# A decoder layer with a mixture of experts: biases fetched as four rows and spread on VectorE, and a fifth list of blocks

## The chip, the core and the metric

The kernel runs on one core of a Trainium2 chip, as one program with one launch. The metric is the device time of that core in microseconds (us); the time given is the median of three runs. A profile is one execution recorded by the hardware, with start and length of the instructions of each engine: PE (TensorE's matrix products; its weight loads are listed apart as PEld), DVE (VectorE), ACT (ScalarE), POOL (GpSimd) and SP (SyncE, which here only issues transfers).

## The reference

One decoder layer in float32, with a layer norm after each of its three parts:

```python
x = layernorm(x + attention(x))        # causal, 16 heads of 128, D = 512, x is 8 x 112 x 512
x = layernorm(x + cross(x, ctx))       # linear attention over ctx (8 x 375 x 512), sigmoid gate
x = layernorm(x + experts(x))

def experts(h):                        # 896 tokens
    logits = h @ router_weight.T + router_bias          # 8 experts
    top_vals, top_idx = top_k(logits, 2)
    top_w = softmax(top_vals)                           # two scores a token
    gate_up = h @ gate_up_proj[e] + gate_up_bias[e]     # 512 -> 1024
    gate, up = gate_up[..., ::2], gate_up[..., 1::2]
    gate, up = minimum(gate, 7), clip(up, -7, 7)
    act = (up + 1) * gate * sigmoid(1.702 * gate)
    y_e = act @ down_proj[e] + down_proj_bias[e]        # 512 -> 512
    return sum over the token's two experts of score * y_e
```

A gate or up bias is a vector of 512 along the columns, and so is the down bias. In the kernel the tokens lie on the 128 partitions, so each of these vectors is needed in every partition that holds a token of its expert.

## The kernel before, in words

The 896 tokens are seven tiles of 128. The work goes through three phases: the self-attention up to about 400 us, the linear cross-attention up to about 720 us, and the experts from there to the end.

**Routing and lists.** As a tile finishes the cross-attention, `close(t)` adds it to the residual, normalises it, finds its two experts (`route`) and writes its rows by indirect DMA to `store`, a buffer in device memory grouped by expert. `upto` keeps the counts. `list_blocks(i)` is a chain of some twenty small VectorE operations that turns the counts into two lists: which expert each step works on (`es`, and as integers `eb`), and which block of `store` holds its tokens. `LISTS` says after how many tiles a list is made, and for which steps. Before the change there are four: after five tiles for steps 0 to 2, after six for steps 3 and 4, and after all seven for steps 13 to 17 and for steps 5 to 12. A list made early can only name blocks that are already full.

**Steps.** There are 18. Steps 0 to 4 and 13 to 17 each take one block of 128 rows of one expert. Steps 5 to 12 are paired: 64 rows of one expert on partitions 0 to 63 and 64 rows of another on 64 to 127. Weights stand in four lanes of three 1 MB slabs (`slab[3q]`, `+1`, `+2` for gate, up and down). A paired step uses two lanes. A weight is fetched again only if the lane's expert has changed (`cond`, a flag that the lists give for the steps from 5 on).

**One step.** `project(s, st, 0)` multiplies the block by the gate weights (`gups`, L1120), adds the bias on VectorE (L1128), takes the minimum (L1130) and gives it to ScalarE's sigmoid (L1132). `project(s, st, 1)` does the same with the up weights and forms the product `g` (L1135 to L1139). `transposed_block` turns `g` on PE and copies it out of PSUM on ScalarE (`aT`, L1022). `down` multiplies by the down weights (`yps`, L1147), and adds the down bias times the score on VectorE (L1158). `add_token` (L1185) adds the token itself once, and GpSimd scatters the rows to `parts` (L1164). The loop at L1283 weaves two steps together: step s's gate product, the transposes of step s−1's `g` and of step s+1's tokens (`start`), step s's up product, step s−1's down product.

**Order.** From L1063 on, PE, VectorE, ScalarE and SyncE execute in the order in which the program is written. GpSimd's instructions are placed by the framework. `tick()` advances the chains that are in progress (`close(t)`, later `close_tiles()`) by one piece, so the place where a chain is appended sets where its instructions stand in each engine's order.

**SyncE's queue.** All weights and biases go through it, in written order, with at most eight transfers outstanding. Before the change the biases go with the weights: `fetch_inner` (L927) sends the two weights and then a copy of the 4 KB gate and up bias to all 128 (or 64) partitions of one of four places in `biases` (`BIAS_AT`). `fetch_down_bias` (L966) copies the 2 KB down bias to all partitions of one of two tiles. The inner biases carry the weights' condition except in the steps where a fresh copy is always needed.

**The end.** After step 12's scatter SyncE's queue reads back `parts` into `xn` and `seconds` (L1173, 14 loads of 256 KB). `close_tiles` (L1213) adds the two, collects the statistics of each tile, takes the roots, scales and writes the tiles out. Steps 13 to 17 don't add through `parts` but gather what is there (`gather`, L1189) and write their rows themselves (`write`, L1198). `find_again` (L1244) compares the token numbers of the late steps, with a product on PE (`keys`, L1249), so that a row that comes twice is written once.

Of the kernel before, what the change touches and what calls it, by code (L numbers as in the profile page):

```python
# [10 lines left out]
F32 = mybir.dt.float32  # L11
# [28 lines left out]
LISTS = ((5, slice(0, 3)), (6, slice(3, 5)), (NT, slice(13, 18)), (NT, slice(5, 13)))  # L40
# [6 lines left out]
BIAS_AT = [0, 1, 2, 3, 0] + [1, 3] * 4 + [0, 2, 1, 3, 0]  # L47
# [6 lines left out]
def decoder_layer(ctx: ExitStack, tc: tile.TileContext, t_in: dict, out: bass.AP):  # L54
# [463 lines left out]
    def route(t: int):  # L518
# [32 lines left out]
        if t < LISTS[1][0] - 1:  # L551
            yield
# [143 lines left out]
    with tc.tile_pool(name="cross", bufs=2) as cr:  # L696
# [207 lines left out]
        make_room(free, free[:, 16 * SC :])  # L904
        blocks = store.rearrange("(n p) w -> n p w", p=P)
# [21 lines left out]
        def fetch_inner(s: int, parts_=None):  # L927
# [3 lines left out]
            for i in parts_:  # L931
                _, half = part_of(s, i)
                e = listed(0, s, half, ET.SP, E - 1)
                chosen[i] = e, listed(2, s, half, ET.SP, 1) if s >= EARLY else None
            for k, n in enumerate(("wg", "wu")):
# [7 lines left out]
            for i in parts_:  # L943
                on, _ = part_of(s, i)
                e, cond = chosen[i]
                if s >= PAIRED or (s < EARLY + 2 and i == 1):
                    cond = None
                nc.sync.dma_start(
                    out=biases[on, BIAS_AT[s], :],
                    in_=gubs[bass.ds(e, 1), :].broadcast_to([on.stop - on.start, 2 * I]),  # L950
                    cond=cond,
                )
# [11 lines left out]
        downs = {}  # L964

        def fetch_down_bias(s: int):  # L966
            downs[s] = side.tile([P, D], F32, tag="down_bias", name=f"down_bias_{s}", bufs=2)
            for i, (e, _) in experts_of.pop(s).items():
                on, _ = part_of(s, i)
                nc.sync.dma_start(  # L970
                    out=downs[s][on],
                    in_=t_in["db"][bass.ds(e, 1), :].broadcast_to([on.stop - on.start, D]),
                )
# [15 lines left out]
        def close(t: int):  # L989
# [4 lines left out]
            if t < LISTS[1][0] - 1:  # L994
                yield
            yield from route(t)
            if t == LISTS[0][0] - 1:
                list_blocks(0)
                fetch_inner(0)
                fetch_down(0)  # L1000
                fetch_down_bias(0)
                ahead_x.extend(fetch_tokens(s) for s in range(3))
            elif t == LISTS[1][0] - 1:
# [403 lines left out]
```

## Time and profile before

The median of the three runs is 993.99 us (991.0 to 998.91). The profiled execution took 993.77 us. Its span, from the first instruction to the last, is 992.2 us, and 1.6 us lie around it. The mean granted clock of TensorE is 0.976 of full speed.

The table gives the busy time of each engine by stretch, with the granted clock, the share of time in which the DMA engines were busy, and what they moved.

| stretch (us) | what runs there | PE | DVE | ACT | POOL | clock | DMA | GB/s |
|---|---|---|---|---|---|---|---|---|
| 0 to 400 | self-attention | 389.3 | 148.8 | 89.1 | 81.4 | 1.00 | 0.29 | 103 |
| 400 to 675 | cross-attention | 268.9 | 154.6 | 80.1 | 43.6 | 1.00 | 0.11 | 37 |
| 675 to 720 | its end, with routing | 38.9 | 30.7 | 13.9 | 5.6 | 0.95 | 0.51 | 194 |
| 720 to 757 | steps 0 to 2, last lists | 35.2 | 28.0 | 9.1 | 4.5 | 0.92 | 0.90 | 362 |
| 757 to 814 | steps 2 to 6 | 52.0 | 27.4 | 9.2 | 9.9 | 0.94 | 0.98 | 331 |
| 814 to 852 | steps 7 and 8 | 28.8 | 10.9 | 3.2 | 4.2 | 0.91 | 1.02 | 312 |
| 852 to 912 | steps 9 to 13 | 60.0 | 30.3 | 8.0 | 8.9 | 1.00 | 0.89 | 313 |
| 912 to 966 | steps 14 to 16 | 39.3 | 35.7 | 9.3 | 8.5 | 0.87 | 0.84 | 327 |
| 966 to 992 | step 17 and the end | 12.8 | 14.7 | 5.0 | 7.1 | 0.81 | 0.22 | 74 |

An engine's busy time against the length of its stretch says whether it is the one that sets the pace. PE fills 852 to 912 to the last microsecond. In 814 to 852 and in 912 to 966 it does not. Where the granted clock is under 1, part of the stretch ran at half speed. In the page's groups, `L1128 DVE ... x36 | 24.8, 689 | 73.6 <-PE gups L1120 56.6` reads: 36 instructions of line 1128 on VectorE, 24.8 us of busy time together, 689 ns each; VectorE stood idle 73.6 us in all just before them, and 56.6 us of that ended with a `gups` product of PE. Idle time of an engine that is off the critical path costs nothing.

### The profile page before, as it was taken

The numbers are of one execution on the slowest core, as the hardware profiler recorded it, in microseconds if no ns is written. First come the engines' busy times: TensorE is split into PE (matmuls) and PEld (weight loads), VectorE is DVE, ScalarE is ACT, GpSimd is POOL, SyncE is SP. The second block draws the span as 40 slices with busy tenths as digits, with TensorE's granted clock in tenths as the row PEclk, the third lists the DMA queues.
The fourth block names the chain that finished last, engine by engine and source line by source line (L and its number), as shares of the span: only waits on it lengthen the run. The fifth ranks groups of instructions, "written<-read, shape, count | busy, mean of one in ns | idle before, by whom it ended". The sixth has DMA issues, their size and how long they took to land.

```text
span 992.2 us, 10895 instructions
## 1 busy us (share of the span) xinstructions
PE 925.1 (93%) x3915; PEld 468.3 (47%) x3915; DVE 481.1 (48%) x1053; ACT 226.9 (23%) x394; POOL 173.8 (18%) x239
## 2 busy tenths in 40 slices
PE   7998999999999999999999999999797997899944
PEld 3455644466445655654555455554453432334421
DVE  1356511154213552565413667676776443355675
ACT  1132321033102321322222233333231111011022
POOL 3133300032001413120002222220111210111112
PEclk9999999999999999999999999999988999899977
DMA  9994004101011001130001020210898999889961
GB/s 350 344 348 183 1 1 169 43 20 66 0 43 43 1 1 43 43 105 10 22 0 31 8 71 9 75 32 22 318 375 305 351 354 307 260 298 400 398 227 64
DMA packets 39653, 142.35 MB, mean 143 GB/s; under 512 B 4438, under 2 KB 8598, under 8 KB 29744
## 3 DMA queue, kind: packets, MB, share of 16 engines
q1 hardware_dynamic: 34176, 126.34, 35.8%
q0 software_dynamic: 4768, 14.98, 4.3%
q8 instruction: 31, 0.51, 0.2%
q10 hardware_dynamic: 656, 0.35, 0.1%
q14 instruction: 22, 0.18, 0.1%
HBM read 135.74 MB, written 30.06 MB: 167 GB/s over the span
## 4 chain that ended last, share of the span: by engine, by line
PE 61%; DVE 13%; issue 12%; DMA 9%; ACT 2%; POOL 1%; POOLq 0%; SPq 0%; DVEq 0%; ACTq 0%
PE ops L254 10%; PE vps L344 6%; DMA parts<-y,nums 5%; PE zps L452 3%; PE xqps L888 2%; PE xgps L888 2%; DVE z L861 2%; PE sps L404 2%; PE xops L254 1%; DMA down_bias<-in_db_dram 1%; PE pps L444 1%; DVE p L429 1%; PE sumps L823 1%; DVE kf L783 1%; PE kvps_0a L769 1%
## 5 line engine op out<-in xcount | busy, mean ns | idle before, releaser
L1120 PE MATMUL gups<-slab,bT 128*64 128x512 f32 (+1 forms) x416 | 136.2, 603 | 2.6 <-DMA slab<-in_wu_dram 1.4
L254 PE MATMUL ops<-slab,zT 128*128 128x512 f32 x224 | 97.9, 593 | 0.0
L1147 PE MATMUL yps<-slab,aT 128*64 128x512 f32 (+1 forms) x208 | 74.4, 650 | 14.5 <-ACT aT L1022 9.9
L1120 PEld LDWEIGHTS gups<-slab,bT 128*64 128x64 f32 (+1 forms) x416 | 48.7, 160 | 73.2 <-issue 68.8
L254 PEld LDWEIGHTS ops<-slab,zT 128*128 128x128 f32 x224 | 42.0, 190 | 50.3 <-issue 49.5
L292 POOL TENSOR_TENSOR ws<-slab 128x256 f32<-128x256 f32 x16 | 11.7, 729 | 281.0 <-PE qk_5c L308 83.0
L1128 DVE TENSOR_TENSOR gu<-gups,biases 128x512 f32<-128x512 f32 x36 | 24.8, 689 | 73.6 <-PE gups L1120 56.6
L344 PE MATMUL vps<-slab,x0T 128*112 128x512 f32 x128 | 59.2, 618 | 1.0 <-DVE x0T L204 0.8
L1147 PEld LDWEIGHTS yps<-slab,aT 128*64 128x64 f32 (+1 forms) x208 | 27.1, 173 | 55.9 <-issue 38.5
L1132 ACT ACTIVATE sg<-gu 128x512 f32<-128x512 f32 x18 | 11.3, 629 | 171.7 <-DVE gu L1130 171.6
L261 DVE TENSOR_TENSOR xn<-xn,ops 128x512 f32<-128x512 f32 x28 | 19.2, 684 | 55.5 <-PE ops L254 55.5
L1164 POOL DMA_INDIRECT parts<-y,nums x16 | 16.5, 1033 | 158.8 <-DVE y L1185 144.2
L452 PEld LDWEIGHTS zps<-pT,v 112*128 112x128 f32 x256 | 33.5, 192 | 12.3 <-issue 11.2
L459 DVE COPY zT<-zps 128x448 f32<-128x448 f32 x32 | 20.0, 624 | 39.8 <-PE zps L452 39.8
L344 PEld LDWEIGHTS vps<-slab,x0T 128*112 128x112 f32 x128 | 23.0, 185 | 31.7 <-issue 30.0
L428 DVE TENSOR_REDUCE nm<-p 112x4 f32<-112x448 f32 x32 | 19.7, 616 | 30.5 <-POOL p L418 30.5
L452 PE MATMUL zps<-pT,v 112*128 112x112 f32 x256 | 33.4, 273 | 0.0
L254 PE MATMUL xops<-slab,gate 128*128 128x512 f32 x56 | 25.7, 602 | 7.1 <-DVE gate L863 7.1
L580 POOL DMA_INDIRECT store<-xn,rows x14 | 14.0, 999 | 86.9 <-DVE count L620 57.5
L1158 DVE SCALAR_TENSOR_TENSOR y<-down_bias,score,yps 128x512 f32<-128x512 f32 x17 | 12.7, 747 | 32.6 <-PE yps L1147 24.6
L404 PE MATMUL sps<-k,q 128*112 128x112 f32 x256 | 28.0, 262 | 0.0
L412 ACT ACTIVATE p<-sps 112x448 f32<-112x448 f32 x32 | 17.4, 544 | 45.6 <-PE sps L404 45.6
(804 smaller groups left out, 1606.9 us busy)
## 6 DMA issues: line engine op xcount, KB each, us to landing
slab<-in_wg_dram SPq DMA_DIRECT2D x26, 1024.0 KB
slab<-in_wu_dram SPq DMA_DIRECT2D x26, 1024.0 KB
slab<-in_wd_dram SPq DMA_DIRECT2D x26, 1024.0 KB
store<-slab SPq DMA_DIRECT2D x8, 1806.0 KB
cT<-in_ctxT_dram SPq DMA_DIRECT2D x8, 750.0 KB
biases<-gubs SPq DMA_DIRECT2D x10, 512.0 KB
slab<-in_wq_dram SPq DMA_DIRECT2D x4, 1024.0 KB
slab<-in_wk_dram SPq DMA_DIRECT2D x4, 1024.0 KB
```

The lines of the kernel that those rows point to most:

```text
L254: nc.tensor.matmul(ps, aT[:, c, t * P : (t + 1) * P], w[:, c, :], start=(c == 0), stop=(c == C - 1),)
L261: nc.vector.tensor_add(xn[:, t, :], xn[:, t, :], ps)
L344: nc.tensor.matmul(ps[:S, :], xT[:, c, b * S : (b + 1) * S], w[:, c, :], start=(c == 0), stop=(c == C - 1),)
L404: nc.tensor.matmul(ps[:S, i * S : (i + 1) * S], qk["q"][:, rows], qk["k"][:, rows], start=True, stop=True,)
L428: nc.vector.tensor_reduce(nm, p, AX.X, ALU.max, negate=True)
L452: nc.tensor.matmul(zps[:, i * S : (i + 1) * S], v[:, half * 4 + i, hl * DH : (hl + 1) * DH], pT[:, i * S : (i + 1) * S], start=True, stop= ...
L459: nc.vector.tensor_copy(zT[:, hl, half * HALF : (half + 1) * HALF], zps[:, :HALF])
L861: nc.vector.reciprocal(zf, zf)
L888: nc.tensor.matmul(ps[:, :HALF], w[:, c, g * P : (g + 1) * P], xT[:, c, cols], start=(c == 0), stop=(c == C - 1),)
L1120: nc.tensor.matmul(ps[rows_], st["bT"][:, c, rows_], slab[3 * q + k][:, c, :], start=(c == 0), stop=(c == C - 1),)
L1128: nc.vector.tensor_add(a, ps, st["bias"][:, k * I : (k + 1) * I])
L1147: nc.tensor.matmul(ps[rows_], st["aT"][:, c, rows_], slab[3 * q + 2][:, c, :], start=(c == 0), stop=(c == C - 1 and s < STEPS - 1),)
```

## The change

**Biases.** The tables `BIAS_AT` and `downs` go. All biases of step s are now fetched by `fetch_biases(s)`: for each expert of the step one row of 4 KB to two (paired) or four partitions, one in each group of 32 (partitions 0, 32, 64 and 96), and a row of 2 KB likewise. They go into parts of the `biases` tile: two places for inner biases, four for down biases. They carry no condition. `spread_biases(s)` then copies, in place, the first partition of each group of 32 to the other 31, with VectorE's shuffle under a mask of zeros: one instruction on 128x1024 and one on 128x512. Two memsets on GpSimd clear the places when the tile is made, before `prepare_pair(2)`.

**Order of the transfers.** `fetch_inner` no longer sends biases. At the top of loop step s, `fetch_biases(s + 1)` is asked for, ahead of the weights that step s issues; step 0's come after step 1's up weights. The spread for step s + 1 stands at the end of loop step s, step 0's ahead of its first product.

**Lists.** The first list is split: step 0 is listed after four tiles, steps 1 and 2 after five. It is one more chain of 21 VectorE operations. Step 0's weights are asked for with its list, step 1's gate weights with the second, step 1's up weights later. The places where `close` and `route` compare against `LISTS[1]` now compare against `LISTS[2]`, which keeps its meaning (six tiles).

**The closing.** In loop step 15 the chain `close_tiles()` is appended behind `project(s, st, 1)` instead of ahead of the transposes, so its first piece stands behind the second projection of step 15.

PE's and ScalarE's instructions are the same and in the same order. VectorE has 56 more, GpSimd 3 more, and one of its row writes at the end stands two places later.

```diff
-LISTS = ((5, slice(0, 3)), (6, slice(3, 5)), (NT, slice(13, 18)), (NT, slice(5, 13)))
+LISTS = (
+    (4, slice(0, 1)),
+    (5, slice(1, 3)),
+    (6, slice(3, 5)),
+    (NT, slice(13, 18)),
+    (NT, slice(5, 13)),
+)
...
+        nc.gpsimd.memset(biases[:, 0, :], 0.0)
+        nc.gpsimd.memset(free[:, 16 * SC :], 0.0)
...
-            for i in parts_:
-                on, _ = part_of(s, i)
-                e, cond = chosen[i]
-                if s >= PAIRED or (s < EARLY + 2 and i == 1):
-                    cond = None
-                nc.sync.dma_start(
-                    out=biases[on, BIAS_AT[s], :],
-                    in_=gubs[bass.ds(e, 1), :].broadcast_to([on.stop - on.start, 2 * I]),
-                    cond=cond,
-                )
...
-        def fetch_down_bias(s: int):
-            downs[s] = side.tile([P, D], F32, tag="down_bias", name=f"down_bias_{s}", bufs=2)
-            for i, (e, _) in experts_of.pop(s).items():
-                on, _ = part_of(s, i)
-                nc.sync.dma_start(
-                    out=downs[s][on],
-                    in_=t_in["db"][bass.ds(e, 1), :].broadcast_to([on.stop - on.start, D]),
-                )
+        flat = biases.rearrange("p q n -> p (q n)")
+
+        def inner_bias(s: int):
+            return flat[:, s % 2 * 2 * I : (s % 2 + 1) * 2 * I]
+
+        def down_bias(s: int):
+            at = 4 * I + s % 4 * D
+            return flat[:, at : at + D]
+
+        def fetch_biases(s: int):
+            for to, of in ((inner_bias(s), gubs), (down_bias(s), t_in["db"])):
+                for i, (e, _) in experts_of[s].items():
+                    on, _ = part_of(s, i)
+                    to_ = to[on.start : on.stop : XH]
+                    nc.sync.dma_start(
+                        out=to_, in_=of[bass.ds(e, 1), :].broadcast_to(to_.shape)
+                    )
+
+        def spread_biases(s: int):
+            for b in (inner_bias(s), down_bias(s)):
+                nc.vector.stream_shuffle(b, b, [0] * XH)
...
+            for i, (n, steps_) in enumerate(LISTS):
+                if t == n - 1:
+                    list_blocks(i)
+                    if i == 0:
+                        fetch_inner(0)
+                        fetch_down(0)
+                    if i == 1:
+                        fetch_inner(1, of=(0,))
...
                 steps = [start(0, side, "bT")]
-                fetch_inner(1)
+                fetch_inner(1, of=(1,))
+                fetch_biases(0)
                 fetch_down(1)
-                fetch_down_bias(1)
                 fetch_inner(2)
...
+            if s == 0:
+                spread_biases(0)
+            if s + 1 < STEPS:
+                fetch_biases(s + 1)
             if st:
                 project(s, st, 0)
...
-            if s == STEPS - LATE + 2:
-                chains.append(close_tiles())
             if before_:
                 before_["aT"] = transposed_block(f"aT_{s - 1}", before_["g"], moe, "aT")
...
                 project(s, st, 1)
+                if s == STEPS - LATE + 2:
+                    chains.append(close_tiles())
                 tick()
...
                 fetch_next(s - 1, fetch_down)
-                if s + 1 < STEPS:
-                    fetch_down_bias(s + 1)
                 if s + 3 < STEPS:
                     ahead_x.append(fetch_tokens(s + 3))
+            if s + 1 < STEPS:
+                spread_biases(s + 1)
```

More of the change, by code (lines that the diff above doesn't have):

```diff
@@ L46 @@
 LANES += [(1,), (2,), (3,), (0,), (1,)]
-BIAS_AT = [0, 1, 2, 3, 0] + [1, 3] * 4 + [0, 2, 1, 3, 0]
 LN_EPS = 1e-5
@@ L550, in route @@
         yield
-        if t < LISTS[1][0] - 1:
+        if t < LISTS[2][0] - 1:
             yield
@@ L925, in decoder_layer, with fetch_inner @@
         experts_of = {}
-        def fetch_inner(s: int, parts_=None):
+        def fetch_inner(s: int, parts_=None, of=(0, 1)):
             chosen = experts_of.setdefault(s, {})
@@ L931, in fetch_inner @@
             for i in parts_:
+                if i in chosen:
+                    continue
                 _, half = part_of(s, i)
@@ L934, in fetch_inner @@
                 chosen[i] = e, listed(2, s, half, ET.SP, 1) if s >= EARLY else None
-            for k, n in enumerate(("wg", "wu")):
+            for k in of:
+                n = ("wg", "wu")[k]
                 for i in parts_:
@@ L962, in fetch_down @@
                 )
-        downs = {}
-        def fetch_down_bias(s: int):
-            downs[s] = side.tile([P, D], F32, tag="down_bias", name=f"down_bias_{s}", bufs=2)
-            for i, (e, _) in experts_of.pop(s).items():
-                on, _ = part_of(s, i)
-                nc.sync.dma_start(
-                    out=downs[s][on],
-                    in_=t_in["db"][bass.ds(e, 1), :].broadcast_to([on.stop - on.start, D]),
-                )
+        flat = biases.rearrange("p q n -> p (q n)")
[15 more added lines that the diff above has]
+                nc.vector.stream_shuffle(b, b, [0] * XH)
         def fetch_tokens(s: int):
@@ L993, in close @@
             yield
-            if t < LISTS[1][0] - 1:
+            if t < LISTS[2][0] - 1:
                 yield
             yield from route(t)
[L997 to L1003, printed above, removed]
-                list_blocks(1)
-                ahead_x.append(fetch_tokens(3))
-            elif t == NT - 1:
-                list_blocks(2)
-                list_blocks(3)
+            for i, (n, steps_) in enumerate(LISTS):
[6 more added lines that the diff above has]
+                        fetch_inner(1, of=(0,))
+                    if i < 3:
+                        ahead_x.extend(
+                            fetch_tokens(s) for s in range(steps_.start, min(steps_.stop, NQ))
+                        )
         nums = const.tile([P, STEPS], I32, name="nums")
@@ L1027, in start @@
             xb = ahead_x.pop(0)
-            st = {"x": xb, "bias": biases[:, BIAS_AT[s], :]}
+            st = {"x": xb, "bias": inner_bias(s)}
             st["bT"] = transposed_block(f"bT_{s}", xb, *home)
@@ L1158, in down @@
             nc.vector.scalar_tensor_tensor(
-                y, downs.pop(s), st["score"], ps, ALU.mult, ALU.add
+                y, down_bias(s), st["score"], ps, ALU.mult, ALU.add
             )
@@ L1329, in decoder_layer @@
                 nc.vector.scalar_tensor_tensor(
-                    st["sum"], downs[s], st["score"], st["sum"], ALU.mult, ALU.add
+                    st["sum"], down_bias(s), st["score"], st["sum"], ALU.mult, ALU.add
                 )
```

## The prediction

> **What bounds the kernel now.** I read the busy shares first, then the list of waits, then the last 300 us in order of time, engine by engine; in the fences a timeline row is start, length, engine, line, operation, and in brackets the idle time before it with its releaser.
>
> ```profile
> PE 925.1 (93%) x3915; PEld 468.3 (47%) x3915; DVE 481.1 (48%) x1053; ACT 226.9 (23%) x394; POOL 173.8 (18%) x239
> ...
> DVE gu L1128 <- DMA biases<-gubs: 16.9, 3, 11.5
> ...
> DVE y L1158 <- DMA down_bias<-in_db_dram: 7.1, 1, 7.1
> ...
> SPq L1173 <- DMA parts<-y,nums: 13.7, 1, 13.7
> ```
>
> TensorE is the bound, so only what makes PE wait counts. The expert steps run from 720 us to the end; a paired step takes 11.47 us when nothing is late (first matmuls of steps 10, 11 and 12 at 864.19, 875.66, 887.13). PE waits in these places, in order:
>
> ```profile
> 677.91 1.95 PE L769 MATMUL kvps_10a<-slab,biases 128*125 128x512 f32 x4 [0.24 <-ACT biases L790]
> ...
> 761.99 6.09 PE L1147 MATMUL yps<-slab,aT 128*128 128x512 f32 x8 [5.95 <-ACT aT L1022]
> ...
> 846.37 6.08 PE L1147 MATMUL yps<-slab,aT 128*64 128x512 f32 x13 [3.75 <-DMA slab<-in_wd_dram]
> ...
> 956.21 0.77 PE L1249 MATMUL keys<-sums,allones 128*128 128x128 f32 x2 [13.89 <-DVE closing L217]
> ```
>
> The same places seen from VectorE (first two rows late biases; then a normal step, whose first add waits 1.90 us for PE only; last a late down bias):
>
> ```profile
> 827.00 0.69 DVE L1128 TENSOR_TENSOR gu<-gups,biases 128x512 f32<-128x512 f32 x1 [11.52 <-DMA biases<-gubs]
> ...
> 838.47 0.69 DVE L1128 TENSOR_TENSOR gu<-gups,biases 128x512 f32<-128x512 f32 x1 [3.52 <-DMA biases<-gubs]
> ...
> 867.86 0.69 DVE L1128 TENSOR_TENSOR gu<-gups,biases 128x512 f32<-128x512 f32 x1 [1.90 <-PE gups L1120]
> ...
> 946.60 0.75 DVE L1158 SCALAR_TENSOR_TENSOR y<-down_bias,score,yps 128x512 f32<-128x512 f32 x1 [7.11 <-DMA down_bias<-in_db_dram]
> ```
>
> So there are two stretches where transfers hold PE: steps 7 and 8, and steps 15 and 16. All else in the expert steps is PE back to back, or the 10 us of small list operations on VectorE at 747 to 757.
>
> **Steps 7 and 8: less traffic.** Step 7 begins at 813.71, step 9 at 851.55: 37.84 us where two steady steps take 22.94, so 14.9 us are lost. From 757 to 850 the DMA engines are 100% busy and move 30.34 MB at 326 GB/s. The bias copies issued there are 10 of 256 KB, 3 of 256 KB and 6 of 128 KB: 4.1 MB, some of them skipped by their condition. At 326 GB/s that is 12.6 us, at the best slices' 424 GB/s 9.7 us. The changed kernel sends four rows of 4 KB and 2 KB instead, some 0.02 MB a step. The loss is 12.4 us of waiting and 2.5 us because the matmul group after the 3.75 us wait takes 6.08 instead of 3.60 us. I take the whole 14.9, as 12.6 us of transfers fewer cover 12.4 us of waiting. Bounds: 9.7 at the least if bytes are all that counts, 14.9 at the most, for PE cannot run ahead of its own order. The weights alone (26 MB) then need 80 us of these 93, and step 7's are issued 18 us before use, so nothing else is late next. Biases of step s+1 are asked for as step s begins, behind at most two or three 1 MB weights (2.5 to 3 us each), and are wanted some 11 us later.
>
> A rule of the Trainium skill speaks against such copies (DMA: Bandwidth & Descriptors, "Rules for kernel authors"): under 64 KB one pays mostly overhead, and an outermost dimension below 16 keeps a copy on that many engines at most. The trace of before has no 16 KB copy in this queue, so nothing there confirms or refutes it. If it added 2 us to each landing, an estimate from that page, the 11 us of lead would still hide it; only the late copy of the tail below would be 2 us later, and the sum 2 us more.
>
> **The shuffles.** 18 pairs, 128x1024 and 128x512. No shuffle is in the trace. One-input rows on VectorE: a reduction takes 0.55 us for 384 elements and 0.69 for 512 (L1258), so 1.1 ns an element; 1024 make 1.25, the pair 1.9 us. The faster form (L1130, 0.43 for 512) makes the pair 1.1 us; the slowest row (reciprocal, L861, 2.95 us for 448) would make it 10.1 us. I take 1.9, a plain one-input pass.
>
> The Trainium skill (VectorE: DVE Perf Modes, "The perf-mode tier table (the rule you actually need)") says that a shuffle has only the 1x form and takes about 2400 ns for 2048 elements. An estimate from that page is 1.8 us a pair; the sum below would be 0.2 us less.
>
> In a steady step the pair stands between the last y operation and the next step's first add, where VectorE idles 1.90 us (877.44 to 879.34 in one of them). It fits. If it is a little longer, the add is late, but the sigmoid and the aT copy behind it on ScalarE end 1.9 us before PE's next yps, so up to 3.8 us costs nothing. Two pairs have no such cover. Step 0's stands behind the list made from six tiles, where VectorE has been busy without a break and the add starts at 729.45, 2.6 us after PE was done; behind it wait the layernorm of the last tile and PE's transposes (PE already waits 0.87 us there). Step 2's stands after the long lists, in front of the add at 758.32, and behind that the aT copy for which PE waits 5.95 us. Both cost the pair in full: **+3.8 us** (2.2 to 20).
>
> **The fifth list.** Its 21 small VectorE operations stand after the routing of tile 3, in front of tile 4's residual add at 675.34. The same 21 after six tiles took 725.46 to 729.26: 3.8 us. What waits behind: that add, bn_stats, the square root on ScalarE, and in ScalarE's order the copy for which PE waits at 677.91, already 0.24 us late. PE then runs without a gap to 692, so nothing gives the 3.8 us back. PE's idle time becomes 4.0 us. After 3.75 us idle a group took 6.08 instead of 3.60, after 3.20 us (707.10) it took a normal 3.67; I take the nearer row, +2.5. Sum **+6.3 us** (3.8 to 7.2). The earlier load of step 0's weights buys nothing: no row shows PE or VectorE waiting for weights before 815. The same count of experts, worked through with the reference's routing, gives every step the same expert, so no load appears or goes.
>
> The two GpSimd memsets (128x1024, 128x1072) stand in front of the sums for context pair 2 at 528.85. The first of these was needed by PE at 533.04 and ended at 530.77, so 2.3 us cover them. Rows: 128x128 takes 0.20 us and 128x1 0.10, so 0.9 us each; a two-input 128x1024 takes 2.35. Cost 0, at the most 2.4.
>
> **The tail: a wait changes its place.** SyncE's queue, 919.31 on: 14 loads of xn and seconds (they wait for step 12's scatter), step 17's wg and wu, two wd, and then the next bias. Before, that bias is the down bias of step 14, wanted after yps of step 14; it lands at 946.5. In the changed order it is step 15's biases, and a shuffle wants them before step 15's first add, at 924.8 in the old clock: one step of PE work earlier. When do they land? Ahead of them stand 3.67 + 4.19 MB, without the 0.5 MB bias that stood there. At the 395 GB/s of 920 to 940 that is 19.9 us, and some 2 us go by from issue to landing. The start waits for the scatter issued at 912.4 to 913.4; it landed 5.9 us later, others within 2.7 (least) to 9.6. Now the weights ahead of it are in by about 910 (6 MB issued from 892 on, at 2.5 us each), so I take 3.0: 916.4 + 21.9 = 938.3. The old queue by the same count (8.6 MB from 919.3) would land at 943.1 and did at 946.5, so 942 is the upper bound, and 936.5 the lower.
>
> From there VectorE works without a break, by the rows of 926 to 964: pair 1.9; step 15's adds, sums, keys, two tiles of the closing, 9.8 (12.85 from 926.65 to 939.5 with four tiles, less 3.1); y 1.5; two tiles 3.1; pair 1.9; step 16's first add 1.0; two tiles 3.1; sums and keys 1.5; last tile and statistics 2.3; second add to g 2.4; roots and keys 2.0; four scalings 2.3; y 1.5; pair 1.9. That is 36.2 us to step 17's first add: 974.5, where it stood at 966.14, +8.4. Its second add no longer waits 2.1 us for PE, which is ahead by then. So **+6.3 us** (4.5 to 10). Moving the closing behind the second projection is in this sum; it puts less in front of step 15's second add and more in front of step 16's.
>
> **Sum**, against the profiled execution's own 993.77 us (span 992.2, 1.6 around it; the median of the three runs, 993.99, is the same): −14.9 + 3.8 + 6.3 + 6.3 = +1.5, so **995 us**. What a measurement can tell from no change here is about 1%, 10 us.
>
> **Rivals.**
> 1. Slower: the late wait of step 15. Every us by which its biases land later is one at the end. The kernel is slower than before from a landing at 936.8, by 1% from 946.7. If the queue is no faster than it was and they land at 946.5, the sum is 1003. For: the scatter and 8 MB stand ahead of them by the order of one queue. Against: the queue loses 0.75 MB and starts empty.
> 2. Faster: PE's gaps shrink less elsewhere. If step 15's biases come with little delay (the tail at 0) and the clock stays up at 678: −14.9 + 3.8 + 3.8 = 986; if the list is hidden too, 983. For: waits at L1128 and L1158 add to 24 us, and all are for the copies removed. Against: the order of SyncE's queue.
> 3. The change does not do what it says: the weights fill the queues by themselves and steps 7 and 8 win 5 us only: 1005. For: 28 weight loads are issued in these 93 us. Against: slices of this stretch swing between 219 and 424 GB/s, so the weights alone have room.
> 4. The shuffle is slow, like the reciprocal: 10.1 us a pair on top of 5.5 us of VectorE work makes a paired step 15.6 instead of 11.47, over some twelve steps +50, so 1045 or more.
>
> **Chances.** Forecast 0.50 (988 to 1003), rival 1 0.18, rival 2 0.17, rival 3 0.08, rival 4 0.07. Faster by over 1%: most of rival 2, 0.16. Slower by over 1%: rivals 3 and 4, half of 1 and a little of the forecast, 0.28. Within: 0.56. Range 983 to 1007: it leaves out rival 4 and the ends of the others.
>
> **What would show it.** Right: no VectorE wait for biases in steps 5 to 12, these at 11.5 us each; shuffle rows of 1.25 and 0.69 us; PE idle 4 us before kvps_10a; a wait of 12 to 15 us of the shuffle in front of step 15. Wrong: PE still waiting for weights in step 7 or 8, a shuffle wait in the paired steps, or step 15's shuffle not waiting.

## The result, and the profile after

Over 20 runs of each kernel the changed kernel takes 996.80 us (median; 994.49 to 1001.47) and the kernel before 993.38 us (988.72 to 998.91). The ratio is 1.0035, with a 95% interval of 1.002 to 1.005: 0.35% slower, clear of noise and inside the 1% that counts as no change here. The profiled execution took 996.02 us with a span of 994.0 us (before: 993.77 and 992.2).

The page of the changed kernel, with the busy times, the moved bytes and the new group of shuffles:

```profile
PE 923.5 (93%) x3915; PEld 467.9 (47%) x3915; DVE 516.8 (52%) x1146; ACT 227.0 (23%) x394; POOL 175.7 (18%) x242
...
DMA packets 35062, 130.48 MB, mean 131 GB/s; under 512 B 3862, under 2 KB 8022, under 8 KB 25152
...
L988 DVE STREAM_SHUFFLE biases<-biases 128x1024 f32<-128x1024 f32 (+1 forms) x36 | 35.0, 1025 | 0.0
```

The page of the kernel before has 142.35 MB, so 11.87 MB of copies are gone, and 35 us of shuffles stand on VectorE in their place. VectorE's 93 more rows are 36 shuffles, a row for the mask of each, and the 21 operations of the list. What PE waits for, as the list of waits of the changed kernel has it (in all, times, longest):

```profile
PE keys L1264 <- DVE sums L1321: 19.3, 2, 14.8
PE yps L1162 <- ACT aT L1037: 10.9, 3, 7.7
...
PE kvps_10a L774 <- ACT biases L795: 3.9, 1, 3.9
```

No transfer is left in PE's list between step 0 and the end. What is left there goes back to VectorE, the longest wait through VectorE to the late rows of step 15. In order of time, from PE's timeline:

```profile
681.91 3.62 PE L774 MATMUL kvps_10a<-slab,biases 128*125 128x512 f32 x4 [3.95 <-ACT biases L795]
...
772.42 6.18 PE L1162 MATMUL yps<-slab,aT 128*128 128x512 f32 x8 [7.74 <-ACT aT L1037]
...
939.08 0.77 PE L1264 MATMUL keys<-sums,allones 128*128 128x128 f32 x2 [14.76 <-DVE sums L1321]
```

The first row was at 677.91 with 0.24 us of waiting, the second at 761.99 with 5.95, the third at 956.21 with 13.89, behind the late down bias. And VectorE's timeline at step 0's pair of shuffles and at step 15's (the row of the mask carries the wait):

```profile
736.26 1.29 DVE L988 STREAM_SHUFFLE biases<-biases 128x1024 f32<-128x1024 f32 x1
...
737.46 0.75 DVE L988 STREAM_SHUFFLE biases<-biases 128x512 f32<-128x512 f32 x1
738.08 0.69 DVE L1143 TENSOR_TENSOR gu<-gups,biases 128x512 f32<-128x512 f32 x1
...
934.49 0.01 DVE L988 LOAD_MASK_SELECT biases<-biases  x1 [16.34 <-DMA biases<-gubs]
```

The first products of steps 7, 8 and 9 stand 11.47 us apart, as in steady steps; before the change steps 7 and 8 lost 14.9 us:

```profile
824.23 3.60 PE L1135 MATMUL gups<-slab,bT 128*64 128x512 f32 x16
...
835.70 3.60 PE L1135 MATMUL gups<-slab,bT 128*64 128x512 f32 x16
...
847.17 3.60 PE L1135 MATMUL gups<-slab,bT 128*64 128x512 f32 x16
```

A pair of shuffles takes 1.82 us from the first start to the add behind it. Step 15's pair waits 16.34 us for its rows.

Cut at the same first products, the two profiled executions compare as follows (us):

| stretch | before | after | difference | term of the forecast |
|---|---|---|---|---|
| start to the first product of context pair 10 | 674.08 | 674.37 | +0.3 | none |
| to step 0 | 46.77 | 53.49 | +6.7 | fifth list +6.3 |
| step 0 to step 3 | 47.06 | 50.57 | +3.5 | two uncovered pairs +3.8 |
| step 3 to step 7 | 45.80 | 45.80 | 0.0 | 0 |
| step 7 to step 10 | 50.48 | 34.42 | −16.1 | fewer copies −14.9 |
| step 10 to step 13 | 34.52 | 34.52 | 0.0 | 0 |
| step 13 to the end of the span | 93.49 | 100.83 | +7.3 | late rows +6.3 |
| sum | 992.2 | 994.0 | +1.8 | +1.5 |

Of the +6.7 in the second line, 1.7 us are not shown to be the list's; the first experiments say why.

### The profile page after: what moved, and what is told of

Read it like the earlier page. It is cut to its first block, busy times and chain, and to the rows that moved or that the text cites. A ratio compares the mean times of both kernels' runs of the same rounds, so it can differ in the third digit from the quotient of the medians.

```text
span 994.0 us, 10986 instructions
## 1 busy us (share of the span) xinstructions
PE 923.5 (93%) x3915; PEld 467.9 (47%) x3915; DVE 516.8 (52%) x1146; ACT 227.0 (23%) x394; POOL 175.7 (18%) x242
## 4 chain that ended last, share of the span: by engine, by line
PE 76%; DVE 12%; issue 6%; DMA 3%; ACT 2%; POOL 1%; POOLq 0%; SPq 0%; DVEq 0%; ACTq 0%
PE ops L259 10%; PE gups L1135 10%; PE vps L349 6%; PE yps L1162 5%; PE zps L457 2%; PE xqps L893 2%; PE xgps L893 2%; DVE z L866 2%; PE sps L409 2%; PE xops L259 2%; PE pps L449 1%; DMA sums<-parts,others 1%; DMA parts<-y,nums 1%; DVE p L434 1%; PE sumps L828 1%
## 5 line engine op out<-in xcount | busy, mean ns | idle before, releaser
L1135 PE MATMUL gups<-slab,bT 128*64 128x512 f32 (+1 forms) x416 | 133.0, 602 | 0.0
L1162 PE MATMUL yps<-slab,aT 128*64 128x512 f32 (+1 forms) x208 | 72.0, 630 | 10.9 <-ACT aT L1037 10.9
L1143 DVE TENSOR_TENSOR gu<-gups,biases 128x512 f32<-128x512 f32 x36 | 24.7, 687 | 34.2 <-PE gups L1135 34.0
L988 DVE STREAM_SHUFFLE biases<-biases 128x1024 f32<-128x1024 f32 (+1 forms) x36 | 35.0, 1025 | 0.0
```

Source lines behind the costliest of these rows:

```text
L988: nc.vector.stream_shuffle(b, b, [0] * XH)
L1135: nc.tensor.matmul(ps[rows_], st["bT"][:, c, rows_], slab[3 * q + k][:, c, :], start=(c == 0), stop=(c == C - 1),)
L1143: nc.vector.tensor_add(a, ps, st["bias"][:, k * I : (k + 1) * I])
L1162: nc.tensor.matmul(ps[rows_], st["aT"][:, c, rows_], slab[3 * q + 2][:, c, :], start=(c == 0), stop=(c == C - 1 and s < STEPS - 1),)
```

## The experiments

Each comparison is with runs of the kernel before on the same chip. The last column is the span of the profiled execution.

| kernel | median | before | ratio (95%) | span |
|---|---|---|---|---|
| changed kernel | 996.80 | 993.38 | 1.0035 (1.002 to 1.005) | 994.0 |
| `list_undone` | 990.62 | 994.61 | 0.9967 (0.9949 to 0.9985) | 988.2 |
| `list_alone` | 1001.87 | 994.61 | 1.0085 (1.0051 to 1.012) | 1001.2 |
| `shuffle_twice` | 1011.43 | 994.61 | 1.0175 (1.0144 to 1.0206) | 1008.8 |
| `early_rows` | 980.36 | 994.61 | 0.9864 (0.9833 to 0.9895) | 978.3 |
| `full_copies` | 1016.65 | 995.71 | 1.0233 (1.0184 to 1.0282) | 1013.8 |
| `closing_back` | 998.37 | 995.71 | 1.0025 (1.0002 to 1.0048) | 997.8 |
| `rows_early_four_lists` | 976.52 | 995.71 | 0.9823 (0.979 to 0.9856) | 972.4 |
| `before_early_down` | 990.07 | 995.71 | 0.9947 (0.992 to 0.9974) | 991.5 |
| `pairs_covered` | 991.96 | 995.46 | 0.996 (0.9944 to 0.9977) | 990.3 |
| `rows_early_four_lists_b` | 975.25 | 995.46 | 0.9807 (0.9783 to 0.9831) | 975.0 |
| `pairs_covered_b` | 971.97 | 994.57 | 0.9766 (0.974 to 0.9792) | 971.9 |

And the stretches of the table above, for every profiled execution (us):

| kernel | pair 10 to step 0 | 0 to 3 | 3 to 7 | 7 to 10 | 10 to 13 | 13 to the end |
|---|---|---|---|---|---|---|
| before | 46.77 | 47.06 | 45.80 | 50.48 | 34.52 | 93.49 |
| changed | 53.49 | 50.57 | 45.80 | 34.42 | 34.52 | 100.83 |
| `list_undone` | 49.81 | 50.40 | 45.79 | 34.42 | 34.52 | 99.76 |
| `list_alone` | 51.61 | 50.23 | 45.79 | 48.60 | 34.55 | 95.68 |
| `shuffle_twice` | 53.46 | 56.85 | 46.57 | 34.93 | 34.84 | 108.33 |
| `early_rows` | 53.45 | 50.26 | 45.79 | 34.43 | 34.52 | 86.17 |
| `full_copies` | 53.47 | 50.54 | 45.79 | 49.82 | 34.52 | 105.66 |
| `closing_back` | 56.22 | 50.52 | 45.80 | 34.42 | 34.52 | 102.78 |
| `rows_early_four_lists` | 46.68 | 50.59 | 45.80 | 34.42 | 34.52 | 86.21 |
| `before_early_down` | 49.81 | 46.98 | 45.79 | 48.14 | 34.58 | 92.79 |
| `pairs_covered` | 62.80 | 51.85 | 45.79 | 34.43 | 34.51 | 86.19 |
| `rows_early_four_lists_b` | 49.80 | 50.37 | 45.80 | 34.42 | 34.52 | 86.11 |
| `pairs_covered_b` | 49.81 | 47.26 | 45.79 | 34.42 | 34.52 | 86.16 |

### The fifth list taken back, and alone

```diff
 # list_undone: the changed kernel with
-LISTS = ((4, slice(0, 1)), (5, slice(1, 3)), (6, slice(3, 5)), (NT, slice(13, 18)), (NT, slice(5, 13)))
+LISTS = ((5, slice(0, 3)), (6, slice(3, 5)), (NT, slice(13, 18)), (NT, slice(5, 13)))
...
-                    if i == 1:
-                        fetch_inner(1, of=(0,))
...
-                fetch_inner(1, of=(1,))
+                fetch_inner(1)
...
```

> The changed kernel with the four lists of before (step 0 listed together with 1 and 2 after five tiles, and step 1's gate and up weights asked for together, as before); the bias rows and shuffles stay. Theory: each term stands by itself. The list costs 6.8 us (matrix products of step 0 begin 7.0 us later than before, 0.3 of it from earlier), so the span falls from 994.0 to about 987, some 5 us under the kernel before, and steps 7 and 8 stay free of waits. Rival: the earlier load of step 0's weights gave the queue the lead that steps 7 and 8 live on. Then a wait for weights or biases comes back there and the span stays at 990 or more.

```diff
 # list_alone: the kernel before with
-LISTS = ((5, slice(0, 3)), (6, slice(3, 5)), (NT, slice(13, 18)), (NT, slice(5, 13)))
+LISTS = ((4, slice(0, 1)), (5, slice(1, 3)), (6, slice(3, 5)), (NT, slice(13, 18)), (NT, slice(5, 13)))
...
+                    if i == 0:
+                        fetch_inner(0)
+                        fetch_down(0)
+                        fetch_down_bias(0)
...
```

> The kernel before with only the fifth list added (step 0 listed after four tiles, its weights and its copied biases asked for then); biases copied as before. Theory: +6.8 us for the list and nothing back, so a span of about 999, and still 37 us and more from the start of step 7 to the start of step 9. Rival: the earlier load of step 0 relieves steps 7 and 8 by itself; then these two take under 30 us and the span is 992 or less.

Without the list the span falls by 5.8 us to 988.2, and steps 7 to 10 take 34.42 us, to the hundredth what they take with it. With the list alone the span rises by 9.0 us, and the steps 7 to 10 still take 48.60, 1.9 less than the 50.48 before and far from 34.42. So the rival falls in both directions: step 0's earlier weights do not feed steps 7 and 8. The list is a cost, and no profile shows a later stretch that pays it back. Two rows of PE in the kernel without the list, the second of which was at 681.91 behind 3.95 us of waiting in the changed kernel:

```profile
673.50 1.88 PE L768 MATMUL kvps_10a<-slab,cT 128*125 128x512 f32 x4
...
677.33 1.95 PE L768 MATMUL kvps_10a<-slab,biases 128*125 128x512 f32 x4 [0.24 <-ACT biases L789]
```

The size needs care, because the stretch from pair 10 to step 0 has more than one length for the same kernel (last section). Up to the next gate products (`xops`) the list can be read apart. From pair 10's first product to them it is 33.02 or 33.03 us in every profile without the list (`pairs_covered` aside, where a transfer is late), and with it 38.03 to 38.14 in four profiles, the changed kernel's among them, and 39.44 and 39.48 in two. So the list costs 5.0 to 6.5 us there.

The gate products themselves then took 3.67 us in some profiles and 5.37 in others, and the list does not decide which: without it 3.67 in two and 5.37 in four, with it 3.67 in one and 5.37 in five. The profile before had the short form and the changed kernel's the long one, in this order:

```profile
707.10 3.67 PE L254 MATMUL xops<-slab,gate 128*128 128x512 f32 x8 [3.20 <-DVE gate L863]
```

```profile
712.50 5.37 PE L259 MATMUL xops<-slab,gate 128*128 128x512 f32 x8 [3.21 <-DVE gate L868]
```

That is 1.7 of the 6.7 us between these two. By the ratios to the kernel before, over several runs each, the list costs 6.8 us in the changed kernel, 8.5 us alone, and 4.1 us together with the early rows that follow below, each of these known to a few us.

The 9.0 us of the list alone are 0.7 from ahead of pair 10, 4.8 up to step 0, 3.2 more up to step 3 and 2.2 from the end, where step 13's down weights came 4.68 us late in that execution, less the 1.9 by which steps 7 to 10 were shorter. The 3.2 us stand there without any shuffle: step 0's gate products took 3.68 us instead of 6.17, PE then waited 3.93 us for VectorE instead of 0.87, and the group behind that wait took 5.95 us instead of 3.60. So a stretch of a single profile can be read only against one in which these groups ran alike.

### The shuffles doubled

```diff
             for b in (inner_bias(s), down_bias(s)):
                 nc.vector.stream_shuffle(b, b, [0] * XH)
+                nc.vector.stream_shuffle(b, b, [0] * XH)
```

> The changed kernel with each shuffle executed twice in a row; the second repeats what the first wrote. Theory: a pair (1.9 us) costs in full where VectorE sets the pace: step 0, step 2 and the three pairs of steps 15 to 17, so 5 x 1.9 = +9.5 us, a span of about 1003.5; in the steady steps a second pair fits, because the copy that PE waits for on ScalarE is done 1.9 us early. Rival: a steady step pays too; twelve steps at 1.9 us more add up to 23 us, a span of 1020 or more, and the step period is 13.4 instead of 11.47.

The span is 1008.8, +14.8 instead of the +9.5 of the theory and far below the rival's 1020. From step 3 to step 13 (45.80, 34.42 and 34.52 us, which became 46.57, 34.93 and 34.84) ten steps took 1.6 us more together: the second pair is all but free in a steady step, as said, though with nothing to spare. What the theory had too small are the ends: 6.3 us instead of 3.8 in steps 0 to 2, and 7.5 instead of 5.7 behind step 13; what the surplus behind step 13 comes from stays open. In steps 0 to 2 the doubled pairs of steps 0 and 2 make 4.3 us: PE waits 4.59 instead of 2.41 us in the first row below, and 9.82 instead of 7.74 in front of step 1's down products. Another 1.7 us is the second row, step 1's gate products, which took 3.60 us behind the shorter wait of the changed kernel (mean granted clock 1.00 there, 0.70 here):

```profile
745.36 0.63 PE L528 MATMUL x2T_ps<-ident,xn 128*128 128x128 f32 x4 [4.59 <-DVE is_first L1048]
745.83 5.29 PE L1136 MATMUL gups<-slab,bT 128*128 128x512 f32 x8
```

Step 1's own doubled pair stays hidden: the second add behind it still waits 1.46 us for PE. VectorE in a steady step with both pairs:

```profile
868.71 1.34 DVE L989 STREAM_SHUFFLE biases<-biases 128x1024 f32<-128x1024 f32 x1
...
870.73 0.73 DVE L989 STREAM_SHUFFLE biases<-biases 128x512 f32<-128x512 f32 x1
871.35 0.68 DVE L1144 TENSOR_TENSOR gu<-gups,biases 128x512 f32<-128x512 f32 x1
...
873.92 0.69 DVE L1144 TENSOR_TENSOR gu<-gups,biases 128x512 f32<-128x512 f32 x1 [0.97 <-PE gups L1136]
```

The add for which PE was done at 869.2 starts at 871.35, yet the second add still waits 0.97 us for PE: the delay ends there.

### The copies put back in the new places

```diff
-                    to_ = to[on.start : on.stop : XH]
+                    to_ = to[on]
```

> The changed kernel with each bias row copied from memory to all partitions of its half, as before the change, at the new places of the queue; the shuffles stay and repeat what is there. That puts 0.75 MB a step back into the queue, unconditionally, and changes nothing else. Theory (bytes): steps 7 to 9 lived on the 4 MB that left the queue, so waits of 10 to 20 us come back between the start of step 7 and the start of step 10 (34.4 us in the changed kernel, 50.5 before), and the span is 1004 or more. Rival (place): the biases were late because of where they stood in the queue and of their condition; then steps 7 to 9 stay near 34.4 us and the span is under 998.

The stretch from step 7 to step 10 is back at 49.82 us (34.42 with rows, 50.48 before), and the span is 1013.8. So what is carried decides; neither the place in the queue nor the condition does. The tail is 4.8 us longer as well (105.66 against 100.83). The waits, in VectorE's list, now stand at the shuffle, which is the first to want the biases:

```profile
DVE biases L988 <- DMA biases<-gubs: 38.6, 6, 13.7
```

Here 144.19 MB are moved in 40214 packets, 13.7 MB and 5152 packets more than with rows. Bytes and packets come back together, so this run does not tell which of the two counts.

### The rows of steps 15 and 16 asked for earlier

```diff
+        late_bias = side.tile([P, 2 * I], F32, name="late_bias")
+        nc.gpsimd.memset(late_bias, 0.0)
         def inner_bias(s: int):
-            return flat[:, s % 2 * 2 * I : (s % 2 + 1) * 2 * I]
+            if s == STEPS - 2:
+                return late_bias
+            n = s % 2 if s < STEPS - 1 else 0
+            return flat[:, n * 2 * I : (n + 1) * 2 * I]
...
             if s == STEPS - LATE - 1:
+                fetch_biases(STEPS - 3)
+                fetch_biases(STEPS - 2)
                 for t in range(NT):
...
-            if s + 1 < STEPS:
+            if s + 1 < STEPS and s + 1 not in (STEPS - 3, STEPS - 2):
                 fetch_biases(s + 1)
```

> The changed kernel with the bias rows of steps 15 and 16 asked for before the 14 loads of xn and seconds instead of behind them and behind 5 MB of weights; step 16's inner rows get a place of their own (one more memset on GpSimd), step 17's take the one of step 14. Theory: the 16.3 us that the shuffle for step 15 waits are due to its place in SyncE's queue alone. They go, and VectorE's unbroken work of 52 us from there sets the end: 16 us less at the most, a span of 978 to 982. Rival: the loads of xn and seconds or the down weights of step 15 are as late as the biases and take their place; then 6 us or less are won, a span of 988 or more. If the place in the queue had nothing to do with it, the span stays at 994.

The median is 980.36 us, 1.4% faster than the kernel before, and the span 978.3 is inside the theory's 978 to 982. VectorE's timeline at step 15, where 16.34 us of waiting stood:

```profile
916.36 0.75 DVE L1208 SCALAR_TENSOR_TENSOR y<-xblk,is_first,y 128x512 f32<-128x512 f32 x1
917.04 0.01 DVE L994 LOAD_MASK_SELECT biases<-biases  x1
917.04 1.32 DVE L994 STREAM_SHUFFLE biases<-biases 128x1024 f32<-128x1024 f32 x1
...
919.01 0.69 DVE L1149 TENSOR_TENSOR gu<-gups,biases 128x512 f32<-128x512 f32 x1
```

The shuffle follows the last operation of the step before without a gap. PE's longest wait of the end is 7.64 us now, at 942.33, for the keys from VectorE, which is busy 53.65 of the 66 us from 912 to 978. So the stretch from step 13 to the end is 86.17 us, 7.3 shorter than before the change, and most of what is left is VectorE's own work.

### The closing in its old place

```diff
+            if s == STEPS - LATE + 2:
+                chains.append(close_tiles())
             if before_:
                 before_["aT"] = transposed_block(f"aT_{s - 1}", before_["g"], moe, "aT")
...
                 project(s, st, 1)
-                if s == STEPS - LATE + 2:
-                    chains.append(close_tiles())
```

> The changed kernel with the chain of the closing appended where it was before, ahead of the transposes of step 15, so its first two tiles (3.1 us) stand before step 15's second add again. Theory: from step 15's shuffle on VectorE works without a break, so the order of the pieces doesn't change the sum: 994 within 1. Rival: PE waits for the second add's result (its keys and the down product stand behind it) and the 3.1 us show: 996 to 997.

The stretch from step 13 to the end is 102.78 against 100.83 us, 1.95 more, and the rest of the 3.8 us by which the span is longer is the stretch ahead of step 0. Counted from step 15's shuffle, which starts at 936.30 here and at 934.49 in the changed kernel, the end of the span is 61.5 and 59.5 us away. VectorE's timeline has the difference at step 17's second add, which follows without a wait in the changed kernel (971.33):

```profile
975.66 0.69 DVE L1143 TENSOR_TENSOR gu<-gups,biases 128x512 f32<-128x512 f32 x1 [2.12 <-PE gups L1135]
```

So VectorE does not work without a break, as the theory had it, and in these two profiles the new place of the closing is worth 2.0 us, not the rival's 3.1. The medians do not show it: the ratios to the kernel before, 1.0025 and 1.0035, have intervals that overlap.

### The old down bias moved forward, in the kernel before

```diff
             if s == STEPS - LATE - 1:
+                fetch_down_bias(s + 2)
                 for t in range(NT):
...
-                if s + 1 < STEPS:
+                if s + 1 < STEPS and s != PAIRED:
                     fetch_down_bias(s + 1)
```

> The kernel before with one move: the copied down bias of step 14 is asked for ahead of the 14 loads of xn and seconds, instead of behind them and behind 5 MB of weights. Theory: the queue's order is what hurts in the tail of both kernels; VectorE's 7.1 us wait for that bias goes and with it 5 to 7 us, a span of 985 to 987. Rival: behind the bias the next transfer is as late (the down weights of step 15), and 2 us or less are won, 990 or more.

The ratio 0.9947 (0.992 to 0.9974) is 5.3 us less, inside the theory's 5 to 7. The profiled execution is one of the longer ones, with a span of 991.5 us that misses the theory's 985 to 987. It shows where the next wait can come from, step 13's down weights, a transfer that the moved copy doesn't touch:

```profile
923.79 6.49 PE L1147 MATMUL yps<-slab,aT 128*128 128x512 f32 x8 [5.10 <-DMA slab<-in_wd_dram]
```

The wait of 7.11 us for the down bias is gone. So the order in the queue hurt the kernel before too. It can be mended without rows and shuffles, but less was won: 5.3 us here, 13.5 us by `early_rows`.

### Both gains together, and the pairs moved

`rows_early_four_lists` is `early_rows` with the four lists of `list_undone`.

> Both gains together: the four lists of before (5.8 us less in the run that undid the fifth) and the rows of steps 15 and 16 ahead of the loads of xn and seconds (15.7 us less). Theory: the two places have nothing to do with each other, so a span of 972 to 974. Rival: VectorE's work of the end is the bound behind both and the loads are no earlier; then 975 or more.

972.4 us of span, 976.52 us median, a ratio of 0.9823: the two gains add up (21.6 us of span against 5.8 and 15.7), though this profile has the short form of the stretch ahead of step 0 and the repetition, at 975.0, the long one. Then the two pairs of shuffles that nothing covers were moved in it.

```diff
 # pairs_covered: rows of step 0 asked for behind its gate and up weights,
 # spread behind the first block's start; step 2's spread ahead of step 1's second add
                     if i == 0:
                         fetch_inner(0)
+                        fetch_biases(0)
...
                 steps = [start(0, side, "bT")]
+                spread_biases(0)
                 fetch_inner(1)
-                fetch_biases(0)
...
-            if s == 0:
-                spread_biases(0)
...
             if st:
+                if s == 1:
+                    spread_biases(2)
                 project(s, st, 1)
...
-            if s + 1 < STEPS:
+            if s + 1 < STEPS and s != 1:
                 spread_biases(s + 1)
```

> The kernel with four lists and early rows, and the two uncovered pairs of shuffles moved to where VectorE waits for PE: step 0's behind the first block's start (2.3 us idle there), with its rows asked for behind step 0's gate and up weights; step 2's ahead of step 1's second add (1.9 us idle). Theory: the pairs of steps 0 and 2 cost 3.4 us where they stood and nothing there, a span of 969. Rival: VectorE's chain from 718 to 743 and from 753 to 769 is what sets PE's waits, and the moved pair only takes idle time from the front of the same chain: 971 or more.

A miss: 990.3 us, some 16 us slower than the kernel it was made from. Step 0's place for the down row lies in memory that the sums of the context pairs use until pair 11, and the row was asked for only with step 0's list (701.57), behind 2 MB of weights. A product of pair 11 had to wait for its landing. PE's timeline:

```profile
710.39 2.04 PE L768 MATMUL kvps_11a<-slab,biases 128*125 128x512 f32 x2 [16.75 <-DMA biases<-in_db_dram]
```

Step 2's moved pair won nothing either: its rows were asked for at 752.81, behind the weights issued ahead of them, and the shuffle could start only at 763.84, after 2.01 us of waiting for them. Both are matters of transfers, not of VectorE. The second try takes only the inner row of step 0, whose place is free, gives step 2's inner row the extra place of step 16 (not shown below), and asks for them ahead of the weights (the second argument picks the inner row, 0, or the down row, 1; the down row's shuffle stands at the end of step 0):

```diff
                         fetch_inner(0)
-                        fetch_biases(0)
+                        fetch_biases(0, (0,))
...
-                spread_biases(0)
+                spread_biases(0, (0,))
+                fetch_biases(0, (1,))
...
                 if s == 0:
+                    fetch_biases(2)
                     fetch_down(2)
```

> The kernel with four lists and early rows once more, on the same chip as the one with the moved pairs, for the comparison of the two: 974 to 979 as before.

> The moved pairs again, without what went wrong in the first try: only step 0's inner row (its place is not used by the context pairs) is asked for behind its gate and up weights, its down row where it was, with its shuffle (0.7 us) at the end of step 0. Step 2's rows get the extra place that step 16 uses later, and are asked for ahead of the 6 MB of weights of loop step 0, so that they are there when VectorE waits for PE in step 1. Theory: the two pairs cost about 3 us where they stood: from the first product of step 0 to that of step 3, 50.4 us with four lists and early rows, it takes 47 to 48, and the span is 3 us shorter, 970 to 972. Rival: the chain on VectorE only gives back idle time in front of it, and this stretch stays at 50.

The stretch from step 0 to step 3 falls from 50.37 to 47.26 us (47.06 before the change, without any shuffle). The median is 971.97 us against 975.25 and 976.52 for the same kernel with the pairs where they were: the pairs cost 3.1 us there, and next to nothing where VectorE waits for PE anyway. This is the fastest version found: 2.3% under the kernel before (0.974 to 0.9792), 2.7% under the changed one by the ratio of the two ratios.

## Why the prediction was right

995 us was forecast, 996.8 was measured, and the four terms of the sum are each where they were put, with sizes off by at most 1.2 us. That they add up to +1.5 us as forecast is in part luck: the gain was 1.2 us too small in the forecast, and two of the losses were too small by 1.4 us together. The medians differ by 3.4 us and the two profiles by 1.8; the stretch ahead of step 0 alone varies by 3.

- **Steps 7 and 8: 14.9 forecast, 16.1 measured.** The mechanism is shown: with the copies back the loss is back, with the list taken out it doesn't move, and with the list alone it shrinks by 1.9 us only. The term was too small because I cut at the start of step 9; that step's own period was still 12.64 instead of 11.47 us, its first products slow (852.29: 4.02 us for 15 instead of 3.60 for 16, mean granted clock 0.93 from 851.55 to 856.25), which adds 1.2. The split of the 14.9 into 12.4 us of waiting and 2.5 us of a slow group was read wrongly. PE's rows there show 9.2 us of idle time; the other 5.7 us are groups that took longer, the slow one among them. The sum doesn't depend on the split.
- **The pairs of steps 0 and 2: 3.8 forecast, 3.5 measured,** and 3.1 won back by moving them. The pair of 1.9 us from a reduction's 1.1 ns an element was 1.82 us. The shuffle's rows are 1.29 and 0.75 us. That the steady steps would hide it held, and nearly so for another pair of the same length (0.16 us a step). The page of the Trainium skill (VectorE: DVE Perf Modes, "The perf-mode tier table (the rule you actually need)") that gives a shuffle one form and about 2400 ns for 2048 elements agrees with these rows: 1.2 us between two starts for 1024. By that figure the forecast's sum would have been 0.5 us less, not 0.2, as three more pairs stand in the chain of the tail.
- **The fifth list: 6.3 forecast, 6.7 between the two profiles.** The mechanism held, the agreement is partly luck. VectorE is 3.7 us later, PE idles 3.95 us in front of pair 10, and the group behind it took 3.62 instead of 1.95 us: 1.7, where the forecast had 2.5 from another row. With 0.3 us regained that is 5.1 us up to the gate products. The rest is the gate products' slower clock in that execution, which comes without the list too. Other profiles with the list have 5.0 to 6.5 us up to there. Nothing gave it back.
- **The tail: 6.3 forecast, 7.3 measured.** Step 15's rows landed at 934.49. Moved by the 5.5 us that the kernel was ahead of the old one by then, that is 940.0 on the clock of the old trace, where I had 938.3, and later than the 936.8 from which the kernel is slower; this is rival 1's mechanism, in the size of the forecast. The first of the 14 loads went out 1.1 us earlier than forecast (909.79, which is 915.3 on that clock); from there the rows took 24.7 us, where 21.9 were forecast. VectorE's chain from their landing to step 17's first add took 35.2 us, where 36.2 were added up from rows. The run with the rows asked for earlier shows that the place in the queue is the whole cause of the wait.

One step of the reasoning was closer to its edge than I saw. The rows were to be hidden by 11 us of lead behind two or three weights. Step 14's took 13.7 us from issue (894.50) to the shuffle's start (908.16), which waited 1.57 us for them; the step itself still took 11.5 us. Step 8's shuffle waited too, 0.49 us at 837.97, at no cost to PE: a shuffle wait in a paired step, which the forecast had named as a sign of being wrong, in a size that stayed hidden. The rule of the Trainium skill against small copies (DMA: Bandwidth & Descriptors, "Rules for kernel authors") was not tested by itself: in no run did a row's own time show apart from what stood ahead of it in the queue.

The forecast's faster rival named the two places at which the change loses most, the list and the tail's queue, and put them at 9 to 12 us together. Without them some 20 us were won (972.4 and 975.0 us of span against 994.0), because the earlier rows take away the whole wait of the end and not only the part that the change added.

## What to carry to other kernels

Where transfers hold PE, as in steps 7 and 8 with the DMA engines 100% busy, copies taken out of the queue give their time back (16.1 us here). But a small copy pays for the queue it stands in, 12.4 us from issue to use for step 15's row: ask for what the next step needs ahead of megabytes that are wanted later, and check that its place is free that early. A pair of shuffles of 1.8 us was all but free where VectorE waits for PE, and cost nearly all of its length where a chain on VectorE sets PE's waits; the idle column of one steady step and of each transition tells which. When a change moves the time little, cut both traces at the same products: here a gain of 16 us and three losses of 17.5 lay behind a difference of 2.

## What the runs showed of the hardware

The stretch ahead of step 0 has two lengths, 3 us apart, for the same program. The products behind a wait of 3.21 us ran at full clock in one execution (mean granted clock 1.00) and below it in another (0.67), two profiles of one and the same kernel, the first from `rows_early_four_lists`, the second from its repetition:

```profile
707.21 3.67 PE L253 MATMUL xops<-slab,gate 128*128 128x512 f32 x8 [3.21 <-DVE gate L862]
```

```profile
707.00 5.37 PE L253 MATMUL xops<-slab,gate 128*128 128x512 f32 x8 [3.21 <-DVE gate L862]
```

Step 0 began at 720.86 in the one and at 723.78 in the other. Among the kernels with four lists the stretch is 46.7 or 46.8 us in two profiles and 49.8 in four, `pairs_covered` aside. Behind the same wait of 3.20 or 3.21 us, three of all the profiles have the short form of these products and nine the long one. The six times of `rows_early_four_lists` fall into two groups, 973.7 to 974.3 and 978.8 to 979.6 us, further apart than these 3 us; what else differs in them no profile here shows. The Trainium skill (TensorE: Matmul & The Clock Gate, "Part 1: The HAM clock gate") describes a free-running activity window of about 3.4 us, after whose idle the clock is halved, and a dependence on its phase from run to run; a wait of 3.21 us that ends either way agrees with the dependence on the phase. Taken by the letter, though, this wait is shorter than one window, and the clock was lower behind it in nine profiles of twelve. For the reader of a profile it means that 3 us between two single executions of this kernel say nothing until the same stretch has been seen twice.

The pair of shuffles works in place on 128 partitions, and the row of the mask that goes ahead of each takes 0.01 to 0.05 us.
